# Four graph layers on one core: the variance from scaled squares, and softmax divisors applied to the attend's result

## The chip, the core and the metric

The kernel runs on 1 core of one Trainium2 chip. Its time is the device time of one execution in microseconds (us); several executions are given by their median. TensorE (PE) does the matmuls and writes PSUM, which has 8 banks; VectorE (DVE) and ScalarE (ACT) read PSUM and SBUF; GpSimd (POOL) works on SBUF here; SyncE (SP) issues nearly all DMAs.

## The reference

The input x has 128 batches of 128 nodes with 512 features, float32. Each of four layers is wrapped in a residual layernorm. `adj` is a sparse 128 x 128 matrix.

```python
x = _layernorm(x + adj @ x @ W0 + bias0)                      # layer 0
h = x @ W1                                                    # layer 1: graph attention
e = leaky_relu(s1[:, :, None] + s2[:, None, :]) * adj         # s1, s2 = h @ a1, h @ a2
x = _layernorm(x + elu(softmax(e, axis=2) @ h + beta * h))
A = adj @ x; C = A + b                                        # layer 2, edge maximum
x = _layernorm(x + max over the last axis of relu(A[:, :, None, :] + (C - A)[:, :, :, None]))
q, k, v = x @ w_qkv, 8 heads of 64                            # layer 3: masked attention
p = softmax(where(adj == 0, -inf, q @ k.T / 8))
o = (p @ v) @ w_proj + b_proj
x = _layernorm(x + o + (layernorm(o) * gamma + beta3))
```

The layernorm has eps = 1e-5. In layer 2 the value added is one number for each node (the maximum over the features of `adj @ x` plus b, at least 0).

## The kernel before

Every batch is a chain of steps in Python (`batch`, a generator), and so are the steps shared by two batches (pairs: `layer0`, `layer1`, `projection`) or four (groups: `section`, `tiled`). A chain asks for an engine with an assumed duration (`use("ACT", 0.48)`), for arena buffers of 256 columns (105 units; `SIZES` and `CAPS` say how large and how many of a kind) and for PSUM banks. A planner (`Plan`) runs all chains against each other when the program is built and emits the instructions of each engine in the order that this gives. Nothing is reordered on the chip: each engine executes its fixed list, and waits where a semaphore is not yet set. The constants at the top (ranks, `SLACK`, `LATE`, `RUN`, `SUMS3`, `SOON`, `KEPT`) bend this order. `RUN` holds a batch until the group that many before it has its layer-3 input; `SUMS3` is the rank of the additions that prepare sums of the layer-3 weights on POOL; a lower rank goes first. `KEPT` is how many last batches stay in SBUF and are not spilled to HBM between the layers.

The products with 512 x 512 weights use a seven-product scheme in place of eight (`seven`): POOL makes differences of input blocks (L919), PE multiplies 128 x 256 pieces (L932 for pairs, L981 for groups), ACT and DVE bring them out of PSUM (L823, L817, L811, L829). The first 14 batches and the last 4 use plain products in some places.

A layernorm is `layernorm_sums`: the row sum comes out of the step before it as an accumulator; DVE negates the mean (L346, L348), ACT squares and sums (L351), ACT divides and adds eps (L353), POOL takes the power -0.5 (L317), ACT multiplies mean and root (L356) and normalizes (L357). It runs four times a batch, but for the very last.

Layer 3 after the scores (L1060, one bank for four heads): DVE adds the mask as it reads PSUM (L1252), takes the maxima of 8 heads (L1260); ACT takes the 8 exps with their sums (L1274); DVE inverts the sums (L1281) and divides the last two heads (L1283), ACT the other six (L1289); DVE transposes 32 x 32 blocks (L1293), and the probabilities go through HBM to finish the transpose (`p_d`, L433 and L437). `attends` (L1081) then leaves the heads' result, transposed, in one bank: a partition is a feature of a head, a column is a node. ACT copies it out (L1324), which frees the bank, and the projection follows. `tiled` puts on PE, without a gap, the scores of two batches, the attends of an earlier group's four, and the scores of two more.

Of the kernel before, what the change touches and what calls it, by code (L numbers as in the profile page):

```python
# [19 lines left out]
APART = 4  # L20
FIRST = 0
PAIRS = 2
SOON = (-2, 2, -4, 10, 6, 18)
WHOLE = 0
KEPT = 6
ATTENDS = 2
RUN = 6
SEVEN0 = 1
SUMS2 = 1
SUMS0 = 0  # L30
SUMS3 = 12
ATTENDS_FIRST = 0
SCALED = 6
# [7 lines left out]
PROJ = -6  # L41
# [3 lines left out]
H = 8  # L45
# [10 lines left out]
CAPS = {"x": 9, "xr": 2, "yT": 8, "v": 4, "qk": 10, "xT": 4}  # L56
SIZES = {"u": 1, "t": 2, "x": 2, "early": 2, "xr": 2, "yT": 2, "v": 4, "qk": 4, "xT": 4}
LAST, AHEAD = 20, 4
# [3 lines left out]
LATE = 1.6  # L62
HANDOFF = {"PE": 0.2, "DVE": 0.13, "ACT": 0.16, "POOL": 0.09, "SP": 0.05}
DVE_ = 1.0
ACT_ = 1.02
POOL_ = 1.0
SP_ = 1.1
# [172 lines left out]
def gnn_stack_kernel(  # L240
# [90 lines left out]
    def layernorm_dve(xb):  # L331
        mv, rstd = yield from mean_rstd(xb)
        yield use("DVE", 0.59)
        nc.vector.tensor_scalar(xb, xb, mv[:, 0:1], rstd, op0=ALU.subtract, op1=ALU.mult)

    def row_sums():

        n = small.tile([P, 7], F32, name="sums", bufs=16)
        return [n[:, c : c + 1] for c in range(7)]

    def layernorm_sums(xb, total, unread, pieces=2):

        total, nm, squares, ve, rstd, nmr, more = total
        yield use("DVE", 0.07, follow=True)
        if unread or pieces == 1:
            nc.vector.tensor_scalar(nm, total, -1.0 / D, None, op0=ALU.mult)  # L346
        else:
            nc.vector.tensor_scalar(nm, total, more, -1.0 / D, op0=ALU.add, op1=ALU.mult)  # L348
        got = yield use("ACT", 1.03, lambda: () if unread else ("t",))
        unread = unread or got  # L350
        nc.scalar.activation(buf_or_bank(unread), xb, AF.Square, bias=nm, accum_out=squares)  # L351
        give(unread)
        nc.scalar.activation(ve, squares, AF.Identity, bias=eps, scale=1.0 / D)  # L353
        yield from root(ve, rstd)
        yield use("ACT", 1.03)
        nc.scalar.activation(nmr, nm, AF.Identity, scale=rstd)  # L356
        nc.scalar.activation(xb, xb, AF.Identity, bias=nmr, scale=rstd)  # L357
# [86 lines left out]
    eps = const.tile([P, 1], F32, name="eps")  # L444
    nc.gpsimd.memset(eps, EPS)
# [200 lines left out]
    class Group:  # L646


        def __init__(self, first, size):
# [10 lines left out]
            self.heads, self.o, self.sc, self.scratch = {}, {}, {}, {}  # L660
            self.eT, self.xT, self.slot, self.left = {}, {}, {}, {}
# [365 lines left out]
    def tiled(gr, before, bs):  # L1027
        yield gr.qk
        waiting = list(range(before.size)) if before else []
        for b in waiting:  # L1030
            yield before.rows[b]

# [33 lines left out]
    def attend(gr, bs):  # L1066
        for b in bs:
            yield gr.rows[b]
        slots = yield use(
# [40 lines left out]
    def batch(i):  # L1110
# [16 lines left out]
        if SEVEN0 and not direct:  # L1127
# [7 lines left out]
            gr.biased[h][j], gr.total[h][j] = biased, (total[0], total[6])  # L1135
# [3 lines left out]
            yield from layernorm_sums(xb, total, None)  # L1139
# [69 lines left out]
        yield from layernorm_sums(xb, total, unread)  # L1209
# [9 lines left out]
        yield use("DVE", 0.12)  # L1219
        nc.vector.tensor_scalar(mx, mx, b2_sb, 0.0, op0=ALU.add, op1=ALU.max)  # L1220
        if SUMS2:
            yield use("ACT", 0.71)
            total = row_sums()
            nc.scalar.activation(xb, xb, AF.Identity, bias=mx, accum_out=total[0])
            yield from layernorm_sums(xb, total, None, 1)
        else:
            yield use("ACT", 0.61)
            nc.scalar.activation(xb, xb, AF.Identity, bias=mx)
            yield from layernorm_dve(xb)
# [48 lines left out]
        short = (1.0 - SCALED / H) * 1.13  # L1278
        yield use("DVE", 0.18 + short + 0.11 * (SCALED < H), port=0.18 + short if short else None)
        rs = small.tile([P, H], F32, name="rs3")  # L1280
        nc.vector.reciprocal(rs, sums)  # L1281
        if SCALED < H:
            nc.vector.tensor_tensor(  # L1283
                pr[:, SCALED:], pr[:, SCALED:],
# [258 lines left out]
```

## Time and profile before

| | us |
|---|---|
| median of 3 runs | 2962.75 (2962.27 to 2963.49) |
| the profiled execution | 2962.69 |
| its span, first to last instruction | 2960.9 |
| PE, DVE, ACT, POOL busy | 2932.6, 2334.8, 2390.1, 1832.6 |
| granted TensorE clock, mean | 0.998 |

Busy time is the union of an engine's instructions. DMA engines are busy 53% of the span over all queues, moving 430.32 MB. A group's mean duration can be longer than the time between its neighbours' starts, because an instruction may begin before the one ahead of it has reported its end; matmuls of 128 x 256 are reported at 380 ns, and eight of them take 1.73 us.

### The profile page before, as it was taken

Reading aid. Unit: us, or ns where it says so; the run is one execution under the profiler, and the core shown is the slowest. Engines: PE = TensorE matmul, PEld = TensorE weight load, DVE = VectorE, ACT = ScalarE, POOL = GpSimd, SP = SyncE. Lnnn points to the kernel's source line nnn. Section 1 sums busy time; section 2 is a strip of 40 time slices with the busy share of each in tenths; the row PEclk is TensorE's granted clock in tenths of the full one; section 3 lists DMA queues with packets and bytes.
Section 4 is the critical chain, followed back from the end, with each engine's and each line's share of the span. In section 5 each row is a group of like instructions: output and inputs, shape, how many; then the busy total and the mean of one; then the engine's idle time right before and its main releaser. Section 6 shows DMA issues by size and latency. Waiting matters only on the chain. (4 is left out here: it accounts for less than half of the span.)

```text
span 2960.9 us, 55267 instructions
## 1 busy us (share of the span) xinstructions
PE 2932.6 (99%) x16503; PEld 2476.2 (84%) x16503; DVE 2334.8 (79%) x5758; ACT 2390.1 (81%) x7430; POOL 1832.6 (62%) x2045
## 2 busy tenths in 40 slices
PE   9999999999999999999999999999999999999998
PEld 5788888888888888888888888888888888888886
DVE  6897778787878778877878788777778778887767
ACT  5789868887877888887887888888888787887967
POOL 7854655574655665655666576665667566574545
PEclk9999999999999999999999999999999999999999
DMA  6535555463654564655545473654556547464435
GB/s 229 124 91 145 161 145 148 135 176 83 172 160 127 159 159 131 168 142 146 156 128 156 121 196 109 178 139 133 167 142 171 128 124 182 136 161 112 126 86 161
DMA packets 879882, 430.32 MB, mean 145 GB/s; under 512 B 567904, under 2 KB 781536, under 8 KB 879584
## 3 DMA queue, kind: packets, MB, share of 16 engines
q1 hardware_dynamic: 861152, 393.23, 49.4%
q10 hardware_dynamic: 18432, 33.56, 3.0%
q8 instruction: 133, 2.18, 0.3%
q14 instruction: 165, 1.35, 0.2%
HBM read 222.10 MB, written 204.54 MB: 144 GB/s over the span
## 5 line engine op out<-in xcount | busy, mean ns | idle before, releaser
L919 POOL TENSOR_TENSOR arena<-arena 128x256 f32<-128x256 f32 (+1 forms) x864 | 746.2, 870 | 387.8 <-PE ps L932 101.6
L317 POOL TENSOR_TENSOR sums<-sums,neghalf 128x1 f32<-128x1 f32 x511 | 329.2, 645 | 530.7 <-ACT sums L353 523.5
L932 PE MATMUL ps<-wsum_sb,arena 128*128 128x256 f32 x2196 | 543.8, 380 | 7.4 <-POOL arena L919 3.0
L932 PEld LDWEIGHTS ps<-wsum_sb,arena 128*128 128x128 f32 x2196 | 413.1, 190 | 89.4 <-issue 20.8
L981 PE MATMUL ps<-arena,wqkv_sb 128*128 128x256 f32 (+1 forms) x2112 | 479.4, 373 | 0.2 <-POOL arena L919 0.2
L932 PE MATMUL ps<-w_sb,arena 128*128 128x256 f32 x1936 | 478.9, 379 | 0.5 <-ACT arena L823 0.5
L823 ACT COPY arena<-ps 128x256 f32<-128x256 f32 (+1 forms) x892 | 336.2, 394 | 159.3 <-PE ps L932 78.2
L981 PEld LDWEIGHTS ps<-arena,wqkv_sb 128*128 128x128 f32 x2112 | 392.1, 190 | 65.1 <-issue 13.2
L351 ACT ACTIVATE arena<-arena,sums 128x512 f32<-128x512 f32 x497 | 355.5, 715 | 96.4 <-DVE sums L346 54.8
L817 DVE TENSOR_TENSOR arena<-ps,arena 128x256 f32<-128x256 f32 (+1 forms) x669 | 292.2, 452 | 176.8 <-ACT arena L823 89.3
L357 ACT ACTIVATE arena<-arena,sums 128x512 f32<-128x512 f32 x511 | 415.8, 814 | 17.1
L932 PEld LDWEIGHTS ps<-w_sb,arena 128*128 128x128 f32 x1936 | 366.0, 190 | 72.0 <-issue 19.9
L1274 ACT ACTIVATE arena<-arena,nmx 128x128 f32<-128x128 f32 x1024 | 402.9, 400 | 2.9 <-DVE nmx L1260 2.7
L981 PE MATMUL ps<-arena,wsum_sb 128*128 128x256 f32 (+1 forms) x1584 | 358.6, 373 | 1.1 <-POOL arena L919 1.1
L981 PEld LDWEIGHTS ps<-arena,wsum_sb 128*128 128x128 f32 x1584 | 293.3, 190 | 50.6 <-issue 7.9
L1289 ACT ACTIVATE arena<-arena,rs 128x128 f32<-128x128 f32 x768 | 278.3, 401 | 5.7 <-DMA x_d<-arena 1.1
L981 PE MATMUL ps<-wqkv_sb,arena 128*128 128x256 f32 x1024 | 241.3, 379 | 0.0
L363 POOL TENSOR_TENSOR arena<-arena,beta_sb 128x512 f32<-128x512 f32 x128 | 171.8, 1343 | 105.4 <-DVE arena L1235 97.8
L932 PE MATMUL ps<-wproj_sb,arena 128*128 128x256 f32 x992 | 236.1, 382 | 0.0
L1163 DVE SCALAR_TENSOR_TENSOR arena<-arena,wa_rows 128x512 f32<-128x512 f32 x256 | 208.4, 822 | 32.2 <-ACT arena L357 28.6
L981 PEld LDWEIGHTS ps<-wqkv_sb,arena 128*128 128x128 f32 x1024 | 194.1, 190 | 33.3 <-issue 6.0
L932 PEld LDWEIGHTS ps<-wproj_sb,arena 128*128 128x128 f32 x992 | 186.1, 190 | 31.5 <-issue 3.7
(117 smaller groups left out, 5375.1 us busy)
## 6 DMA issues: line engine op xcount, KB each, us to landing
p_d<-arena SPq DMA_DIRECT2D x256, 256.0 KB
arena<-p_d SPq DMA_DIRECT2D x128, 512.0 KB
x_d<-arena SPq DMA_DIRECT2D x242, 256.0 KB
arena<-x_d SPq DMA_DIRECT2D x968, 64.0 KB
arena<-in_x SPq DMA_DIRECT2D x127, 256.0 KB
out<-arena ACTq DMA_DIRECT2D x127, 256.0 KB
x_s<-arena SPq DMA_DIRECT2D x122, 256.0 KB
arena<-x_s SPq DMA_DIRECT2D x122, 256.0 KB
```

Of the source, the lines that this page charges most:

```text
L317: nc.gpsimd.tensor_tensor(rstd, ve, neghalf, op=ALU.pow)
L351: nc.scalar.activation(buf_or_bank(unread), xb, AF.Square, bias=nm, accum_out=squares)
L357: nc.scalar.activation(xb, xb, AF.Identity, bias=nmr, scale=rstd)
L363: nc.gpsimd.tensor_tensor(dst, dst, other, op=ALU.add)
L817: nc.vector.tensor_tensor(c, a, c, op=ALU.add)
L823: nc.scalar.copy(c, a)
L919: nc.gpsimd.tensor_tensor(blocks(out), blocks(a), blocks(b), op=ALU.subtract)
L932: nc.tensor.matmul(p, t[:, k], w[:, k, :], start=first and k == 0, stop=final and k == 1, skip_group_check=True,)
L981: nc.tensor.matmul(to, lhs, rhs, start=first and j == 0 and k == 0, stop=final and k == 1, skip_group_check=True,)
L1163: nc.vector.scalar_tensor_tensor(unread, xb, 1.0, wa_rows[:, j, :], op0=ALU.mult, op1=ALU.mult, accum_out=gr.s[:, b, j : j + 1],)
L1274: nc.scalar.activation(pr[:, j, :], pr[:, j, :], AF.Exp, bias=nmx[:, j : j + 1], accum_out=sums[:, j : j + 1],)
L1289: nc.scalar.activation(pr[:, j, :], pr[:, j, :], AF.Identity, scale=rs[:, j : j + 1])
```

## The change

The **variance**: the square is taken of the row scaled by 512^-0.5, with the negated mean scaled alike, so that the accumulator is the variance itself. DVE then adds eps and DVE multiplies mean and root; both were ACT's. **Layer 2**: its row constant is no longer added to the whole row by ACT. The layernorm before it sums its own output while it writes it, and the constant goes into the mean alone (`after`). The **attends** get undivided exps. The inverted sums of two batches are transposed by DVE, written to HBM (`r_d`), and loaded again so that every partition of a head holds that head's divisors along its columns (`divisors`; buffer kind "d", 4 units, one for each pair). DVE multiplies the attend's result by them as it leaves PSUM. The load is issued when all rows of the group are there (`divide`). The last 2 batches (`EARLY`) divide ahead of the attend as all did, four heads on each engine, and have the copy by ACT.

Constants of the planner change as well: weight sums later (`SUMS3`), 9 groups in place of 6 (`RUN`), 8 buffers x in place of 9, 7 batches kept, the last batch's exps in one instruction (`WHOLE`), attends of the last 3 groups apart in place of 4 (`APART`), other ranks and assumed durations.

```diff
-APART = 4
+APART = 3
-SOON = (-2, 2, -4, 10, 6, 18)
-WHOLE = 0
-KEPT = 6
+SOON = (-2, 2, -4, 12, 6, 18)
+WHOLE = 1
+KEPT = 7
-RUN = 6
+RUN = 9
-SUMS2 = 1
+EARLY = 2
-SUMS3 = 12
+SUMS3 = 24
-SCALED = 6
+SCALED = 4
-PROJ = -6
+PROJ = -4
-CAPS = {"x": 9, ...
+CAPS = {"x": 8, ...
-LAST, AHEAD = 20, 4
+LAST, AHEAD = 22, 4
-LATE = 1.6
+LATE = 1.8
-DVE_ = 1.0
+DVE_ = 1.04
-POOL_ = 1.0
-SP_ = 1.1
+POOL_ = 0.98
+SP_ = 1.0
...
+    def layernorm_sums(xb, total, unread, pieces=1, after=None, total_out=None):
+        total, nm, var, rstd, nmr, more = total
+        if after is None:
+            yield use("DVE", 0.07, follow=True)
+            if pieces == 1:
+                nc.vector.tensor_scalar(nm, total, -1.0 / D * D**-0.5, None, op0=ALU.mult)
...
         else:
-            nc.vector.tensor_scalar(nm, total, more, -1.0 / D, op0=ALU.add, op1=ALU.mult)
-        got = yield use("ACT", 1.03, lambda: () if unread else ("t",))
+            yield use("DVE", 0.2, follow=True)
+            nc.vector.tensor_scalar(nm, total, -1.0 / D, after, op0=ALU.mult, op1=ALU.subtract)
+            nc.vector.tensor_scalar(nm, nm, after, D**-0.5, op0=ALU.add, op1=ALU.mult)
+        got = yield use("ACT", 0.72, lambda: () if unread else ("t",))
...
-        nc.scalar.activation(buf_or_bank(unread), xb, AF.Square, bias=nm, accum_out=squares)
-        nc.scalar.activation(ve, squares, AF.Identity, bias=eps, scale=1.0 / D)
-        yield from root(ve, rstd)
-        yield use("ACT", 1.03)
-        nc.scalar.activation(nmr, nm, AF.Identity, scale=rstd)
-        nc.scalar.activation(xb, xb, AF.Identity, bias=nmr, scale=rstd)
+        nc.scalar.activation(
+            buf_or_bank(unread), xb, AF.Square, bias=nm, scale=D**-0.5, accum_out=var
+        )
+        yield use("DVE", 0.07, urgent=True)
+        nc.vector.tensor_scalar(var, var, EPS, None, op0=ALU.add)
+        yield from root(var, rstd)
+        yield use("DVE", 0.07, urgent=True)
+        nc.vector.tensor_scalar(nmr, nm, rstd, D**0.5, op0=ALU.mult, op1=ALU.mult)
+        if total_out is None:
+            yield use("ACT", 0.7)
+            nc.scalar.activation(xb, xb, AF.Identity, bias=nmr, scale=rstd)
+        else:
+            yield use("ACT", 0.78)
+            nc.scalar.activation(xb, xb, AF.Identity, bias=nmr, scale=rstd, accum_out=total_out)
...
-        yield from layernorm_sums(xb, total, unread)
+        sums2 = row_sums()
+        yield from layernorm_sums(xb, total, unread, total_out=sums2[0])
...
-            yield use("ACT", 0.71)
-            total = row_sums()
-            nc.scalar.activation(xb, xb, AF.Identity, bias=mx, accum_out=total[0])
-            yield from layernorm_sums(xb, total, None, 1)
+        yield from layernorm_sums(xb, sums2, None, after=mx)
...
+        for b in waiting:
+            done(before.divide[b // 2])
...
+        if i >= NB - EARLY:
...
+        else:
+            yield use("DVE", 0.12)
+        if i < NB - EARLY and h not in gr.rs:
+            gr.rs[h] = small.tile([P, 2, H], F32, name="rs3", bufs=6)
+            plan.start(divisors(gr, h), i)
+        if i < NB - EARLY:
+            nc.vector.reciprocal(
+                gr.rs[h][:, b % 2].rearrange("p (c j) -> p j c", j=2),
+                sums.rearrange("p (j c) -> p j c", j=2),
+            )
+            done(gr.summed[h])
...
-        nc.scalar.copy(oT, p)
+        if i >= NB - EARLY:
+            p, ba, v = gr.o.pop(b)
+            yield use("ACT", 0.48, urgent=True)
+            nc.scalar.copy(oT, p)
+        else:
+            yield gr.divided[h]
+            p, ba, v = gr.o.pop(b)
+            yield use("DVE", 0.6, urgent=True)
+            nc.vector.tensor_tensor(oT, p, gr.divisor[h][:, b % 2], op=ALU.mult)
+            gr.read(("d", h), 2)
...
+    def divisors(gr, h):
+        yield gr.summed[h]
+        bt = yield use("DVE", 0.62, "t")
+        st = buf(bt, 2, H, S)
+        nc.vector.transpose(
+            st, gr.rs.pop(h)[:, :, :, None].to_broadcast([P, 2, H, S])
+        )
+        row = dram.tile([2 * H, Q, S], F32, name="r_d", bufs=8)
+        yield use("SP", 0.4, late=2.0)
+        nc.sync.dma_start(
+            row.rearrange("e a r -> a e r"), st[::S].rearrange("p b h s -> p (b h) s")
+        )
+        give(bt)
+        if gr.first < firsts[-APART]:
+            yield gr.divide[h]
+        slot = gr.slot["d", h] = yield use("SP", 0.8, "d", late=2.6)
+        gr.divisor[h] = buf(slot, 2, K, P)
+        heads = row.rearrange("(e j) a r -> j e (a r)", j=2)
+        for j in range(2):
+            nc.sync.dma_start(
+                gr.divisor[h][j * HD : (j + 1) * HD].rearrange("p b c n -> p (b c) n"),
+                heads[j][None].to_broadcast([HD, 2 * K, P]),
+            )
+        done(gr.divided[h])
```

## The prediction

> **What bounds the kernel now.** I read the page first, then the waits of TensorE (PE), then the stretches, then the groups of ScalarE (ACT) and VectorE (DVE) by shape, then the timeline of the end. The page's first lines say that PE decides:
>
> ```profile
> span 2960.9 us, 55267 instructions
> ...
> PE 2932.6 (99%) x16503; PEld 2476.2 (84%) x16503; DVE 2334.8 (79%) x5758; ACT 2390.1 (81%) x7430; POOL 1832.6 (62%) x2045
> ```
>
> The reader is to see that PE is covered 99% of the time while no other engine is over 81%. The change touches no matmul, so the 2932.6 us stay. What can be won is PE's uncovered time, 2960.9 - 2932.6 = 28.3 us, and the little that it runs at a lower clock. The waits of PE say how thin this is:
>
> ```profile
> PE ps L1214 <- ACT arena L357: 4.6, 5, 1.7
> PE ps L932 <- ACT arena L823: 3.4, 3, 2.0
> PE ps L932 <- POOL arena L919: 3.0, 2, 1.7
> PE ps L370 <- ACT arena L1324: 1.9, 1, 1.9
> ```
>
> Columns: total us, times, longest. ACT ends most of it: the layernorm's last step (L357), the evacuation (L823), the attend's copy (L1324). The stretches say where; per engine they give the busy us:
>
> ```profile
> 90.00:115.00 25.00, 22.36 (x98) 17.00 (x97) 21.16 (x69) 22.13 (x55) 23.58 (x26) 1.00 0.60 141
> 115.00:145.00 30.00, 26.03 (x109) 20.41 (x108) 25.28 (x80) 25.87 (x68) 25.24 (x29) 0.94 0.42 93
> 200.00:300.00 100.00, 100.00 (x517) 83.31 (x516) 75.94 (x182) 95.01 (x288) 52.42 (x59) 1.00 0.54 145
> 2900.00:2920.00 20.00, 20.00 (x176) 17.69 (x176) 13.98 (x31) 19.08 (x73) 4.56 (x7) 1.00 0.53 160
> 2920.00:2940.00 20.00, 18.00 (x111) 11.63 (x109) 16.96 (x38) 12.01 (x38) 15.88 (x17) 1.00 0.65 196
> ```
>
> The columns are length, then PE, weight load, DVE, ACT, POOL, granted clock, DMA share, GB/s. **Early** (90 to 145 us) PE lacks 2.64 + 3.97 = 6.6 us, and 6% of the clock over 30 us is another 1.8: 8.4 us, with DVE, ACT and POOL all at 84 to 94%. **The end** lacks 2.0 us in 2920 to 2940 and some 1.85 in the next ten. The last matmul ends about 10.3 us before the span does; that tail is last(), which is not edited. The start is 1.4 us. That leaves 28.3 - 1.4 - 6.6 - 3.85 - 10.3 = 6.1 us for the **middle**, over 2700 us. So about 20 us are within reach (8.4 + 6.1 + 3.85 and some 1.7 of slow clock at the end), 0.7% of the time.
>
> The timeline of the end shows the slow clock: the same eight matmuls before and after a wait of 1.86 us.
>
> ```profile
> 2934.49 3.60 PE L370 MATMUL ps<-wproj_sb,arena 128*128 128x512 f32 x8
> ...
> 2941.85 5.40 PE L370 MATMUL ps<-wproj_sb,arena 128*128 128x512 f32 x8 [1.86 <-ACT arena L1324]
> ```
>
> The wait of 1.86 us was followed by 1.8 us of slow matmuls, so a wait here costs up to twice its length. The Trainium skill (TensorE: Matmul & The Clock Gate, Part 1: The HAM clock gate) puts the drop to half rate after an idle window of about 3.4 us; by it waits of 2 us would be free of that second cost, the end would hold 3.85 us and not 5.5, and my gain below would be 0.9 us smaller. The row is what I use.
>
> **The change, part by part.** The groups by shape that I price with (count, busy us, mean ns, idle before):
>
> ```profile
> L1289 ACT ACTIVATE arena<-arena,rs 128x128 f32<-128x128 f32 x768 | 278.3, 401 | 5.7 <-DMA x_d<-arena 1.1 <-DMA arena<-x_d 0.9 <-ACT arena L823 0.8
> L353 ACT ACTIVATE sums<-sums,eps 128x1 f32<-128x1 f32 x511 | 150.5, 294 | 16.6
> L356 ACT ACTIVATE sums<-sums 128x1 f32<-128x1 f32 x511 | 147.8, 289 | 58.9 <-POOL sums L317 56.2 <-ACT arena L823 0.7 <-issue 0.2
> L1224 ACT ACTIVATE arena<-arena,mx 128x512 f32<-128x512 f32 x128 | 91.5, 715 | 22.3 <-DVE mx L1220 20.4 <-DVE logits L764 1.4 <-DVE arena L1163 0.2
> L1324 ACT COPY arena<-ps 128x512 f32<-128x512 f32 x128 | 72.2, 581 | 50.1 <-PE ps L1081 49.9
> ```
>
> *ACT loses* all of L353 and L356 (150.5 + 147.8), L1224's activation (91.5; its accumulator read moves to L357), L1289 but for 8 of its 768 (275) and 126 of 128 copies (71): 736 us, so ACT falls from 2390 to about 1654 us, 56%. Rows of neighbours overlap a little, so less in occupancy, perhaps 670. ACT is off the bound; the worth lies where PE waited for it.
>
> *DVE gains.* Tiny 128x1 instructions are reported at 143 ns (L346) and 206 ns (L1220, with a pointer), but the timeline has their successors start 70 and 130 ns later, which is what they occupy. Per layernorm one of each, the added epsilon and the negated mean times the reciprocal root: 511 x 0.07 = 36 and 511 x 0.13 = 66. Layer 2's mean becomes two instructions, about 0.33 for 0.07: 128 x 0.26 = 33. The attend's result is multiplied as it leaves PSUM, nearest row L1252 (128x512 from PSUM, 680 ns, successive starts about 0.6): 126 x 0.6 = 76. A 128x512 transpose per pair (L1235, 706 ns, about 0.62): 63 x 0.62 = 39. L1283 goes: 128 x 0.42 = -54. Sum +196: DVE 2335 to about 2531 us, 85.5%. Bounds: if the small ones occupied their whole rows, 511 x (0.143 + 0.206) = 178 for 102, 88%; if each hid behind its neighbour, 82%. The Trainium skill (VectorE: DVE Perf Modes, The TRN2 errata) speaks against this step: every small instruction pays a fixed cost, put there at about 150 cycles of 0.96 GHz as measured. By that the 1022 small ones would take some 160 us, an estimate from that page, and DVE would stand at 87.5%. The starts in the trace are closer, so I keep 85.5%.
>
> Does DVE at 85.5% hold PE up? The row of 200 to 300 us has ACT at 95% with PE at 100.00 of 100: an engine nearly full costs nothing when the order is planned ahead of it. Against it, early there is no lead: 18 layernorms run in 90 to 145 (L357's counts, 7 and 11), adding 18 x 0.2 + 5 x 0.26 = 4.9 us to DVE's 46.4 of 55: 93%. ACT falls there by some 12 of 48.
>
> *Early, 8.4 us.* Layernorms lose a queue turn on ACT, and layer 2 goes from the maximum straight to the squares, without L1224's 0.72 us and its accumulator read. SUMS3 = 24 lets the additions of later batches go before the 16 weight sums on POOL (L595; 19.5 of POOL's 38.4 us in 50 to 90), though the sums must still run before the first section; one x buffer less holds a batch back. I take -5; bounds 0 + 8 (DVE full) and -8.
>
> *Middle, 6.1 us.* L357 ends the two longest waits (near 2458 and 140 us); the shorter chain takes 2.5 off. New waits for DVE: +1.5 taken, by the 95% row; bounds 0 and +15.
>
> *End, 5.5 us.* ACT is at 19.08 of 20 in 2900 to 2920; of this stretch's exps and scalings, 24 scalings in 2900 to 2940 (8.6 us) become 8, and the last batch's eight exps become one over the whole tile with two more DVE passes. The last scores' way to the last attend gets 3 to 6 us shorter, worth at most the 5.5: I take -3, bounds 0 and -5.
>
> *Divisors through HBM.* 63 writes and 126 broadcast loads of 256 KB, 32 MB on 430: DMA from 53% to about 57%. SP issues three more per pair at 0.37 to 0.57 us (rows of s_d), 1.3 us in 46. They run beside the probabilities' own way (transposes, p_d out and in) and are priced at nothing while they land before the attend ends. Behind the wait stands DVE's multiplication, in order, and with it every DVE evacuation queued after it; the attend's bank stays held.
>
> Sum: -5 - 2.5 + 1.5 - 3 = -9. The profiled execution took 2962.69 us (1.8 outside its span) and the median is 2962.75: **2953.7, say 2954**. A measurement of this kernel tells 0.2%, 5.9 us, from no change: faster means under 2956.8, slower over 2968.7.
>
> **Rivals.** (1) *Gains and new waits cancel*: early DVE at 93% gives nothing back, the end gives 3, the middle adds 2: 2957 to 2968. For it: POOL at 94% early, which is not relieved as a whole. (2) *Divisors land late, slower*: the load is released only when the group's rows are all there, just before score and attend (1.98 + 3.65 us). p_d's load at 2931.7 had its attend start at 2938.0, 6.3 us. If the broadcast takes as long, the first attends' banks stay some 2.5 us longer, and the multiplication blocks DVE's queue. Where this exceeds what the other banks cover, PE stands; at 0.5 to 1 us for each of 32 groups it is +16 to +32: 2970 to 2986 after the gains at the lower end. It decides from a landing later than 3.8 us after release, when two batches are scored and the first two attended (1.98 + 1.82 us). Against it: the order knows this time and can place other work. (3) *DVE becomes the bound*: its in-order waits add to 85.5%, and early and at the group borders PE waits for evacuations (L817, L829): +15 to +25 against -9, 2969 to 2979. For it: DVE at 89% in 145 to 200 already, though PE was full there.
>
> **How the numbers follow.** Forecast 0.49, its own range 2946 to 2956.8; (1) 0.19; (2) 0.18; (3) 0.14. Faster 0.49, same 0.19, slower 0.32. The range reaches from 2945 (the 20 us nearly all won) to 2983, leaving out the worst third of (2) and a little on top of the gains.
>
> **What would show it.** Right: ACT near 56 to 58%, DVE near 85%, PE's idle in 90 to 145 at 3 us or less, no wait of DVE for DMA at the new multiplication, L370 without its 1.86 us wait. Wrong: waits of PE for DVE over 5 us in all; DVE idle before the multiplication ended by the divisors' DMA; PE's idle in the middle over 10 us.

## The result, and the profile after

The changed kernel takes 2981.6 us (median of 4 runs, 2979.85 to 2985.33) against 2963.12 for the kernel before in the same runs: a ratio of 1.0063, with a 95% interval of 1.0051 to 1.0076. It is slower by 0.6%, where 2954 us had been forecast. The profiled execution took 2979.85 us. The first lines of its page:

```profile
span 2978.1 us, 55051 instructions
...
PE 2936.7 (99%) x16503; PEld 2472.8 (83%) x16503; DVE 2478.5 (83%) x6973; ACT 1766.6 (59%) x5379; POOL 1816.7 (61%) x2044
```

ACT lost 623.5 us and DVE gained 143.7, as planned, and the span still grew by 17.2 us. PE's busy time grew by 4.1, its idle time by 13.1. Where, by stretches of the span (idle us of PE; e1_narrow is an experiment told below):

| | 0 to 90 | 90 to 145 | 145 to 300 | 300 to 2800 | 2800 to end | sum |
|---|---|---|---|---|---|---|
| before | 1.54 | 6.62 | 0 | 6.05 | 14.05 | 28.3 |
| after | 5.26 | 1.14 | 0.44 | 16.65 | 17.94 | 41.4 |
| e1_narrow | 4.62 | 0.54 | 0.37 | 8.33 | 17.86 | 31.7 |

The middle, which had 6 us to give, lost 10.6 more. The waits of PE (total us, times, longest) name what came in:

```profile
PE ps L944 <- POOL arena L931: 6.9, 6, 1.9
PE ps L408 <- DMA arena<-in_x: 6.1, 4, 3.0
PE ps L381 <- ACT arena L1347: 6.0, 1, 6.0
PE ps L1231 <- ACT arena L368: 2.1, 6, 0.8
```

Three things are new against the table of before. PE waits for loads of x (`in_x`, L408), which it never noticeably did. Its wait for POOL's differences (L944 for L931; before, L932 for L919) has grown from 3.0 to 6.9 us. And the wait ahead of the end's L381 (L370 before) has grown from 1.9 to 6.0. The early stretch (90 to 145 us) did what was forecast and better; busy us of PE, weight load, DVE, ACT and POOL, then granted clock, DMA share and GB/s:

```profile
90.00:115.00 25.00, 24.55 (x120) 20.12 (x119) 21.86 (x73) 16.54 (x39) 22.65 (x26) 1.00 0.40 81
115.00:145.00 30.00, 29.31 (x134) 23.61 (x133) 27.29 (x109) 21.49 (x53) 26.45 (x33) 1.00 0.44 103
```

Now one of the new stalls in the middle, from three views of the changed kernel. The timeline of the queue of SP (start us, us), which issues the loads:

```profile
1679.97 4.08 SPq L1392 DMA_DIRECT2D arena<-r_d  x4
1684.14 0.57 SPq L493 DMA_DIRECT2D arena<-in_x  x1
```

The timeline of PE:

```profile
1689.20 1.10 PE L408 MATMUL ps<-arena,adjT 128*128 128x512 f32 x2 [2.98 <-DMA arena<-in_x]
```

And the stretches around it:

```profile
1680.00:1684.00 4.00, 4.00 (x20) 3.52 (x19) 3.21 (x16) 1.97 (x6) 0.93 (x2) 1.00 0.47 149
1684.00:1690.00 6.00, 3.02 (x13) 2.10 (x12) 2.54 (x5) 2.35 (x4) 2.62 (x3) 1.00 1.04 289
```

The four divisor loads of a group (L1392, 4 x 256 KB = 1 MB) go out together. The load of x that a later layer 0 needs stands behind them in the same queue. For 6 us the DMA engines are fully busy (share 1.04, 289 GB/s, where the whole span has a mean of 156), the x arrives late, and PE stands for 2.98 us. No other engine is near full in that stretch, and nobody waits there for the divisors themselves.

A second path may be POOL's. Its waits for the spilled rows, before (L919) and after (L931):

```profile
POOL arena L919 <- DMA arena<-x_d: 31.1, 9, 6.1
```

```profile
POOL arena L931 <- DMA arena<-x_d: 92.5, 17, 16.6
```

These are loads as well. That PE's longer wait for L931 follows from them is a guess at this point. The theory after this reading, **"loads"**: the 32 MB of divisors, issued in bursts of 1 MB, delay the loads queued behind them. Its rival, **"DVE"**: the extra 144 us of in-order work on DVE shifts evacuations and with them everything else. A third, **"order"**: the constants of the planner were fitted to other work, and a different list of instructions is simply a worse list.

### The profile page after: what moved, and what is told of

It reads as the page before. It is cut to its first block, busy times and chain, and to the rows that moved or that the text cites. A ratio compares the mean times of both kernels' runs of the same rounds, so it can differ in the third digit from the quotient of the medians.

```text
span 2978.1 us, 55051 instructions
## 1 busy us (share of the span) xinstructions
PE 2936.7 (99%) x16503; PEld 2472.8 (83%) x16503; DVE 2478.5 (83%) x6973; ACT 1766.6 (59%) x5379; POOL 1816.7 (61%) x2044
## 2 busy tenths in 40 slices
DMA packets 950404, 463.33 MB, mean 156 GB/s; under 512 B 574172, under 2 KB 852316, under 8 KB 950108
## 4 chain that ended last, share of the span: by engine, by line
PE 76%; DVE 8%; POOL 6%; DMA 3%; issue 3%; ACT 2%; SPq 2%; POOLq 0%; ACTq 0%; DVEq 0%
PE ps L993 32%; PE ps L944 28%; PE ps L1074 3%; PE ps L389 3%; PE ps L1231 3%; PE ps L1097 3%; PE ps L408 2%; POOL arena L374 2%; POOL arena L931 2%; POOL sums L317 1%; SPq L430 1%; DMA arena<-in_x 1%; DVE arena L1179 1%; DVE arena L829 1%; PE ps L381 1%
## 5 line engine op out<-in xcount | busy, mean ns | idle before, releaser
L931 POOL TENSOR_TENSOR arena<-arena 128x256 f32<-128x256 f32 (+1 forms) x864 | 725.8, 850 | 477.0 <-DVE arena L1352 112.3
L944 PE MATMUL ps<-wsum_sb,arena 128*128 128x256 f32 x2196 | 543.0, 380 | 8.7 <-POOL arena L931 6.9
L354 ACT ACTIVATE arena<-arena,sums 128x512 f32<-128x512 f32 x497 | 356.9, 718 | 246.0 <-DVE sums L342 98.9
L944 PEld LDWEIGHTS ps<-wsum_sb,arena 128*128 128x128 f32 x2196 | 412.9, 190 | 92.0 <-issue 18.8
L993 PE MATMUL ps<-arena,wqkv_sb 128*128 128x256 f32 (+1 forms) x2112 | 477.9, 373 | 0.0
L944 PE MATMUL ps<-w_sb,arena 128*128 128x256 f32 x1936 | 477.7, 379 | 0.0
L993 PEld LDWEIGHTS ps<-arena,wqkv_sb 128*128 128x128 f32 x2112 | 392.0, 190 | 62.8 <-issue 11.0
L944 PEld LDWEIGHTS ps<-w_sb,arena 128*128 128x128 f32 x1936 | 365.7, 190 | 68.6 <-issue 16.5
L365 ACT ACTIVATE arena<-arena,sums 128x512 f32<-128x512 f32 x383 | 307.6, 812 | 155.0 <-DVE sums L362 136.7
L993 PE MATMUL ps<-arena,wsum_sb 128*128 128x256 f32 (+1 forms) x1584 | 355.2, 373 | 0.4 <-POOL arena L931 0.3
L993 PEld LDWEIGHTS ps<-arena,wsum_sb 128*128 128x128 f32 x1584 | 293.1, 190 | 46.0 <-issue 6.2
L993 PE MATMUL ps<-wqkv_sb,arena 128*128 128x256 f32 x1024 | 242.0, 379 | 0.3 <-DVE arena L823 0.3
L944 PE MATMUL ps<-wproj_sb,arena 128*128 128x256 f32 x992 | 239.2, 382 | 1.0 <-DVE arena L1352 1.0
L993 PEld LDWEIGHTS ps<-wqkv_sb,arena 128*128 128x128 f32 x1024 | 193.9, 190 | 32.9 <-issue 5.2
L1179 DVE SCALAR_TENSOR_TENSOR arena<-arena,wa_rows 128x512 f32<-128x512 f32 x256 | 210.5, 829 | 10.2 <-ACT arena L365 4.5
L944 PEld LDWEIGHTS ps<-wproj_sb,arena 128*128 128x128 f32 x992 | 185.3, 190 | 33.6 <-issue 4.2
L374 POOL TENSOR_TENSOR arena<-arena,bproj_sb 128x512 f32<-128x512 f32 x124 | 163.2, 1325 | 68.6 <-ACT arena L835 56.2
L1284 ACT ACTIVATION_READ_ACCUMULATOR arena<-arena,nmx 128x1 f32 x1016 | 199.4, 196 | 0.0
```

Of the source, the lines that this page charges most:

```text
L374: nc.gpsimd.tensor_tensor(dst, dst, other, op=ALU.add)
L931: nc.gpsimd.tensor_tensor(blocks(out), blocks(a), blocks(b), op=ALU.subtract)
L944: nc.tensor.matmul(p, t[:, k], w[:, k, :], start=first and k == 0, stop=final and k == 1, skip_group_check=True,)
L993: nc.tensor.matmul(to, lhs, rhs, start=first and j == 0 and k == 0, stop=final and k == 1, skip_group_check=True,)
L1179: nc.vector.scalar_tensor_tensor(unread, xb, 1.0, wa_rows[:, j, :], op0=ALU.mult, op1=ALU.mult, accum_out=gr.s[:, b, j : j + 1],)
L1284: nc.scalar.activation(pr[:, j, :], pr[:, j, :], AF.Exp, bias=nmx[:, j : j + 1], accum_out=sums[:, j : j + 1],)
```

## Experiments

The difficulty is that the order is planned when the program is built: a changed assumed duration anywhere gives another list. So the sharpest kernels here keep the list of the changed kernel (or of before) and change only the size of an operand, the layout or the queue of a transfer, or add one. In e1, e5, e10, e11 and e13 the traces hold the instructions of every engine in the same order as in the changed kernel; so do e9 and e12 (e12 against the kernel before), but for the transfers that are moved or added.

**e1_narrow: the same list, less divisor data.** Each load fills 8 partitions of 64; the rest of the divisor tile is not written, so the attend's result is multiplied by stale values.

```diff
-                gr.divisor[h][j * HD : (j + 1) * HD]...
-                heads[j][None].to_broadcast([HD, 2 * K, P]),
+                gr.divisor[h][j * HD : j * HD + 8]...
+                heads[j][None].to_broadcast([8, 2 * K, P]),
```

> The changed kernel with the order of every engine's instructions kept, but each broadcast load of the divisors reaches 8 of its 64 partitions (32 KB in place of 256 KB, 28 MB less in all; the other partitions are multiplied by whatever lies there, so the result is left out of account). Theory DMA (the added transfers delay the loads of x and x_d that stand behind them, and PE ends up waiting for those): PE's waits for arena<-in_x fall from 6.1 us to under 1.5, POOL's wait for arena<-x_d from 92.5 us towards the 31 us of before, PE's idle between 300 and 2800 us from 16.6 to about 7, the time by some 9 us to about 2972. Theory DVE (DVE's 143 us more of work makes PE late): nothing changes, 2980 to 2984. Theory order (the fixed order is simply less lucky): nothing changes either.

Measured: 2968.04 us, ratio to before 1.0018 [1.0008, 1.0027]. That is 13.6 us below the changed kernel; 10.5 between the two profiled spans. The page, and the waits of PE and of POOL:

```profile
PE 2935.9 (99%) x16503; PEld 2476.9 (83%) x16503; DVE 2479.5 (84%) x6973; ACT 1768.5 (60%) x5379; POOL 1820.1 (61%) x2044
```

```profile
PE ps L381 <- ACT arena L1347: 6.0, 1, 6.0
PE ps L944 <- POOL arena L931: 3.8, 3, 1.9
...
PE ps L408 <- DMA arena<-in_x: 1.5, 2, 1.3
```

```profile
POOL arena L931 <- DMA arena<-x_d: 52.0, 12, 14.5
```

DVE is as busy as in the changed kernel, with the same instructions, and the slowdown is gone but for 5 us: this is the loads. The same place in its SP timeline (it falls 4 us earlier), and the 6 us from the issue of x on, which in the changed kernel were those of 1.04:

```profile
1676.47 2.50 SPq L1392 DMA_DIRECT2D arena<-r_d  x4
1679.06 0.36 SPq L493 DMA_DIRECT2D arena<-in_x  x1
```

```profile
1679.00:1685.00 6.00, 6.00 (x28) 4.90 (x27) 4.04 (x11) 3.12 (x6) 3.57 (x4) 1.00 0.77 238
```

The load of x leaves 2.59 us after the first divisor load, not 4.17, and meets DMA engines that are less full. In the landing records of the two traces it then lands 2.90 us after its issue (at 1681.96), not 4.92 (at 1689.06). So at this place 1.6 us of the delay are SP's issue and 2.0 the transfer. Both shrink together: a median load takes SP 304 ns to issue and not 632. How the 13.6 us divide between the two, this kernel doesn't tell.

POOL's waits are a weaker sign than they look. Under the name x_d they fall from 92.5 to 52.0 us, but 12.5 us come up under r_d and 21.3 under the load of e_d; over all loads and stores, POOL waits at L931 for 118.4 us in the changed kernel and 102.8 here. What does fall with the time are PE's own waits.

**e13_half: 32 of the 64 partitions** (the same edit with 32 for 8; the other half stale).

> The changed kernel, same order of every engine, each broadcast load of the divisors to 32 of its 64 partitions (128 KB; the other half is multiplied by what lies there). If the cost grows with the bytes, half of the narrow loads' gain of 13.6 us (which was for 7/8 of the bytes) comes: 4/7 of it, 7.8 us, so 2971 to 2977. If only a whole burst blocks, near 2981; if the number of issues counts and not the bytes, near 2981 too.

Measured: 2969.8 us, 1.0022 [1.0013, 1.0031]. Its wait of PE for x:

```profile
PE ps L408 <- DMA arena<-in_x: 1.2, 2, 0.7
```

Half the bytes give back 11.8 of the 13.6 us, where in proportion it would have been about 8, so the cost is no price per byte. It looks like a threshold: what counts is whether a load that PE needs comes too late, and with the half bursts it mostly does not. Here too both shrink, the bytes and SP's issue (448 ns a load).

**e5_contiguous: the same bytes and list in larger pieces.** The divisors are laid out so that each partition reads one run of 4 KB and not eight of 512 bytes.

```diff
-        heads = row.rearrange("(e j) a r -> j e (a r)", j=2)
+        heads = row.rearrange("(j e) a r -> j (e a r)", j=2)
...
-                heads[j][None].to_broadcast([HD, 2 * K, P]),
+                heads[j][None].to_broadcast([HD, 2 * K * P]),
```

> The changed kernel with the same order of every engine and the same bytes, but the inverted sums are laid down so that the 8 rows of 128 that one partition loads follow each other in HBM: each broadcast load is 64 pieces of 4 KB in place of 512 of 512 B (504 in place of 4032 packets per engine group, 56,000 fewer in all). If what delays the loads behind it is the number of pieces (issue and packets), most of the 13.6 us that the narrow loads won comes back: 2968 to 2973, and PE's waits for arena<-in_x fall under 3 us. If it is the bytes (32 MB through the same 16 engines), nothing moves: 2979 to 2984.

Measured: 2985.4 us, 1.0071 [1.0056, 1.0086], with 893,956 packets in place of 950,404. No gain: the number of pieces is not the cause. (SP's issue hardly changes, 588 ns a load for 632.)

**e12_before_bytes: the opposite direction.** The kernel before, with four extra copies of 256 KB for each group on SP at the place where the group's attends begin (`tiled`), from x to a scratch tensor in HBM that nobody reads: 460.74 MB in all, near the changed kernel's 463.33. DVE, ACT, PE and POOL keep their lists.

```diff
+        for b in waiting:
+            nc.sync.dma_start(dram.tile([P, D], F32, name="none", bufs=16), x[before.first + b])
```

> The kernel before with the divisors' traffic alone: when a group's rows are there, SP issues four copies of 256 KB from the input to a scratch in HBM (31 groups, 32.5 MB) that nobody reads; all other instructions and their order as before. Theory bytes: 8 to 14 us more than before, 2970 to 2977, with PE waiting for arena<-in_x or POOL for arena<-x_d. If the order of before has room for the traffic: within 3 us of 2962.8, and the bytes hurt only where the change's order left the loads late.

Measured: 2971.81 us, 1.0033 [1.0021, 1.0044], 8 us above before; PE's idle in 300 to 2800 us goes from 6.05 to 12.55. Copies in bursts harm the old kernel as well, with nothing else changed, and by some 60% of what the divisors cost in the new one. The way that the expectation gave for it does not show, though. No wait of PE for in_x is over the 0.3 us of before, and POOL's wait for x_d is shorter than the 31.1 us of before:

```profile
POOL arena L919 <- DMA arena<-x_d: 26.7, 10, 5.0
```

PE's idle time grows in small pieces, most of them put down to POOL, ACT and an attend. So e12 shows that such traffic costs time in another list too, and not by which wait.

**e9_act_queue: the divisor loads are issued by ACT**, which has become free, so that x and x_d don't stand behind them on SP.

```diff
-            nc.sync.dma_start(
+            nc.scalar.dma_start(
```

> The changed kernel with the divisors' broadcast loads issued by ACT in place of SP, same bytes, same place in the emission; PE, DVE, POOL and the rest of SP keep their order. If the loads of x and x_d are late because they stand behind the divisors in SP's own queue, most of the 13.6 us that the narrow loads won comes back: 2968 to 2974, PE's waits for arena<-in_x under 2 us. If it is the DMA engines' bandwidth, which all queues share, little moves, and ACT's blocked issue can add: 2978 to 2988.

Measured: 2996.46 us, 1.0120 [1.0103, 1.0137], worse than any expectation. The first two lines are from the waits of PE, the third from those of DVE:

```profile
PE ps L408 <- DMA arena<-in_x: 1.4, 2, 0.8
...
PE ps L1074 <- DVE arena L1352: 4.8, 2, 3.9
```

```profile
DVE arena L1352 <- DMA arena<-r_d: 16.7, 9, 5.6
```

The wait for x falls from 6.1 to 1.4, which fits that a good part of it was the place behind these loads in SP's queue. But the loads now reach the multiplication late (16.7 us of waits, where the changed kernel has 6.6), DVE blocks there, and PE waits for it: here rival (2) of the prediction takes place. Of the 16.3 us that its span is longer than the changed kernel's, 8.1 are idle time of PE; the other 8.2 are PE's busy time, with a mean clock of 0.995 for 0.998. The Trainium skill (DMA: Bandwidth & Descriptors, Rules for kernel authors) says that spreading the issue over several engines doesn't help the bandwidth and only saves issue time; e9, which won nothing by it, does not speak against that, and adds what it costs on the other side: 126 issues of a median 611 ns, by that some 77 us of ACT's queue, in an order that had not planned for them.

**e10_dve_light: the rival "DVE", tested alone.** The multiplication takes one of the attend's four blocks of 128 columns, and the divisors' transpose one head of eight; the rest of the results is left out. Loads and list are unchanged.

```diff
-            nc.vector.tensor_tensor(oT, p, gr.divisor[h][:, b % 2], op=ALU.mult)
+            nc.vector.tensor_tensor(oT[:, :1], p[:, :1], gr.divisor[h][:, b % 2, :1], op=ALU.mult)
...
-            st, gr.rs.pop(h)[:, :, :, None].to_broadcast([P, 2, H, S])
+            st[:, :, :1], gr.rs.pop(h)[:, :, :1, None].to_broadcast([P, 2, 1, S])
```

> The changed kernel with DVE's new large instructions cut down (the multiplication of the attend's result to 1 of 4 feature blocks, the divisors' transpose to 1 of 8 heads; the rest of both is left out), all orders, waits and bytes kept. DVE's busy time falls by some 80 us to about 2400. Theory DVE (its load makes PE late): 5 to 9 us less, 2973 to 2977. Theory bytes: within 2 us of 2981.6.

Measured: 2981.33 us, 1.0062 [1.0047, 1.0077]. Its page, and the stretch of 1500 to 2000 us in it, in the changed kernel, in e1_narrow and in e12_before_bytes:

```profile
PE 2938.7 (99%) x16503; PEld 2474.5 (83%) x16503; DVE 2414.6 (81%) x6973; ACT 1769.0 (59%) x5379; POOL 1819.5 (61%) x2044
```

```profile
1500.00:2000.00 500.00, 493.19 (x2802) 418.74 (x2802) 407.15 (x1181) 289.60 (x869) 304.99 (x350) 1.00 0.58 156
```

```profile
1500.00:2000.00 500.00, 493.17 (x2823) 418.21 (x2822) 418.94 (x1182) 288.52 (x867) 305.06 (x351) 1.00 0.58 155
```

```profile
1500.00:2000.00 500.00, 497.82 (x2853) 424.20 (x2852) 425.93 (x1194) 295.24 (x900) 307.09 (x351) 1.00 0.53 146
```

```profile
1500.00:2000.00 500.00, 498.47 (x2854) 425.96 (x2853) 396.88 (x984) 408.02 (x1289) 319.63 (x357) 1.00 0.58 159
```

64 us less on DVE change nothing: PE stands for 6.8 us of these 500 with or without them, and for 2.2 when the loads are small. So the large new instructions on DVE are not the cause. The 1022 small ones were not taken away in any run with this list; but e1 keeps them all and has lost all but 5 us of the slowdown, so no more than that is left to them.

**The end: e4, e6 and e11.** PE's wait of 5.96 us ahead of the last batches' projection is ended by ACT's copy (L1347). *e4_end_copy_dve* gives this copy to DVE, *e6_end_first* lets the planner put it ahead of two layernorm pairs on ACT, *e11_end_pool_light* has POOL add only a quarter of the columns in the last 8 batches (the other columns keep what they held).

```diff
 e4:
-            yield use("ACT", 0.48, urgent=True)
-            nc.scalar.copy(oT, p)
+            yield use("DVE", 0.6, urgent=True)
+            nc.vector.tensor_copy(oT, p)
 e6:
-        yield use("SP", 0.43, late=4.0)
+        yield use("SP", 0.43, late=4.0 if i < NB - EARLY else 0.0)
 e11, and alike for the addition of o to xs[i]:
+            cut = slice(0, P if i >= NB - 8 else D)
+            plan.start(pool_add(o[:, cut], bproj_sb[:, cut], biased), i)
```

> The changed kernel with the last two batches' copies out of PSUM (L1347) on DVE in place of ACT; the order is the same up to the last 40 us. If PE's wait of 5.96 us at 2957.6 comes from ACT's order (the copies stand behind two layernorm instructions that wait for DVE, while ACT is idle), it falls to 2 us or less and with it the slow clock after it: 4 to 6 us less, about 2976. If the wait comes from DVE and POOL being behind with the last projections, DVE's copy is as late: within 1.5 us of 2981.

> The changed kernel with one assumed duration changed for the last two batches (the landing of their probabilities, 0 in place of 4.0), so that the planner puts their two copies out of PSUM (L1347) ahead of two layernorm pairs on ACT; all engines keep their order until the last 40 us. Theory of ACT's order: PE's wait of 5.96 us for L1347 falls under 1.5 us and the half clock after it shortens: 4 to 7 us less, 2975 to 2978. If PE's gap only moves to the next product, the time stays within 1.5 us of 2981.6.

> The changed kernel with POOL's additions of layer 3 cut to a quarter of their columns for the last 8 batches (the other columns are left out), orders kept; some 13 instructions of 1.3 us become 0.5. If the last 25 us are set by the chain of the last layernorms over POOL and DVE, and PE's wait of 6 us only shows it: 4 to 7 us less, 2975 to 2978. If they are set by PE and ACT's copies: within 1.5 us of 2981.6.

Measured: 2984.32 us, 1.0069 [1.0054, 1.0084]; 2980.7 us, 1.0058 [1.0042, 1.0075]; 2981.84 us, 1.0063 [1.0048, 1.0078]. None moves the time. e6 is the instructive one. The timelines of PE at the end, first of the changed kernel, then of e6 ("..." leaves out the last attends):

```profile
2942.66 7.03 PE L381 MATMUL ps<-wproj_sb,arena 128*128 128x512 f32 x16
...
2957.55 5.17 PE L381 MATMUL ps<-wproj_sb,arena 128*128 128x512 f32 x8 [5.96 <-ACT arena L1347]
2962.55 3.62 PE L1511 MATMUL ps<-wproj_sb,arena 128*128 128x256 f32 x16
```

```profile
2945.61 7.03 PE L381 MATMUL ps<-wproj_sb,arena 128*128 128x512 f32 x16
...
2955.08 3.70 PE L381 MATMUL ps<-wproj_sb,arena 128*128 128x512 f32 x8 [0.54 <-ACT arena L1347]
2958.62 3.62 PE L1511 MATMUL ps<-wproj_sb,arena 128*128 128x256 f32 x16
```

The wait is gone, so it came from the copies' place in ACT's list. Counted from the 16 matmuls of L381 that both have, PE ends 6.9 us earlier: 16.6 us after their start and not 23.5. But the span ends only 0.8 us earlier, 34.6 us after their start and not 35.4, and what comes after the last matmul grew from 11.9 to 18.0 us (10.2 in the kernel before). So the end is hardly set by PE, and PE's longest wait was mostly a sign. From 2940 to 2960 us the changed kernel has DVE and POOL nearly full:

```profile
2940.00:2960.00 20.00, 14.04 (x65) 8.08 (x64) 17.31 (x42) 4.15 (x9) 19.01 (x18) 0.84 0.38 118
```

A lighter POOL alone (e11: 10.0 in the same 20 us) wins no more: its span of 2981.4 us ends 34.5 us after the same matmuls.

```profile
2946.85 7.03 PE L381 MATMUL ps<-wproj_sb,arena 128*128 128x512 f32 x16
```

Which part of the chain of the last layernorms on DVE, POOL and ACT holds the end stays open; no run takes DVE's share of it away.

**The parts alone: e2 and e3.** *e2_variance_alone* sets `EARLY = 128`: every batch divides ahead of the attend, and no divisor goes through HBM (the inverted sums get 8 buffers in place of 2). *e3_attends_alone* keeps the divisors and puts back the layernorm and layer 2 of before.

```diff
 e2:
-EARLY = 2
+EARLY = 128
 e3: layernorm_sums and the code of layer 2 as in the kernel before
```

> The changed kernel with EARLY = 128: every batch divides ahead of its attend as the last two do (four heads on each engine), no divisors go through HBM, the copy is ACT's again; the scaled-square variance, layer 2 and all constants stay. The planner makes another order. Theory DMA: the middle's idle falls by about 10 us, the end stays; 2968 to 2973. Theory DVE: DVE keeps the small instructions and half of the divisions (its busy time close to 2440), so about half of the loss stays: 2972 to 2977. Theory order: anything within 10 us of 2981.

> The changed kernel with the layernorm and layer 2 of before (ACT divides, adds eps, multiplies mean and root, adds the row constant), undivided exps and divisors through HBM kept, all constants of the change kept. Theory DMA: the middle's idle stays at 14 us or more and PE still waits for arena<-in_x; 2978 to 2988. Theory DVE: DVE falls by some 130 us to about 2345 and the middle's idle with it to under 9 us; 2968 to 2974. Theory order: anything within 10 us of 2981.

Measured: 3006.34 us, 1.0144 [1.0123, 1.0165], and 3029.49 us, 1.0224 [1.0209, 1.0239]: each alone is slower than both together, outside every expectation. e2's longest wait of PE is a single one of 14.1 us for `p_d`, and it has one of 4.1 us for `in_x`, with no divisor load at all: another list can have PE wait for x for other reasons. e3 has DVE at 2370.3 us, less than the changed kernel, and is the slowest of all. Neither says what a part is worth: each has another list, with constants that were changed for both parts together.

**How much a list alone is worth: e7, e8, e14 to e18.** To see this, one assumed factor is moved by one or two hundredths (the factor on DVE's assumed durations, 1.04 after and 1.0 before), or a margin of the planner is set to 0.48. The computation stays the same; only the order differs. *e14* is e7's order with e1's narrow loads.

```diff
 e7:  -DVE_ = 1.04  +DVE_ = 1.03        e8:  -DVE_ = 1.0  +DVE_ = 1.01
 e16: -DVE_ = 1.04  +DVE_ = 1.05        e15: -DVE_ = 1.0  +DVE_ = 1.02
 e18: +MARGIN = 0.48 (after)            e17: +MARGIN = 0.48 (before)
```

> The changed kernel with the assumed factor on DVE's durations 1.03 in place of 1.04: the same work in another order, to see how far the order alone moves the time. If the order is of little weight: within 5 us of 2981.6. If the constants were found for just this order: 2985 to 3010.

> The kernel before with that factor 1.01 in place of 1.0, for the same question. If the order is of little weight: within 5 us of 2962.7. If the constants were found for just that order: 2967 to 2990.

> The changed kernel with the assumed DVE factor 1.03 (2992.6 with full loads) and the narrow loads of 8 partitions, so the order is that of e7_replan_after. If the bytes cost in any order: 8 to 15 us less, 2978 to 2985. If they cost only where the first order left the loads late: 2989 to 2994.

> The kernel before with the assumed DVE factor 1.02: a third order of the old work. After 3013 at 1.01, the theory that the constants were found for just one order expects 2980 to 3025; if 1.01 was a single bad draw, 2963 to 2975.

> The changed kernel with the assumed DVE factor 1.05: a third order of the new work. The theory that orders scatter by tens of us whatever the work expects 2985 to 3020; if the new work bears re-ordering better (ACT with room), 2978 to 2995.

> The kernel before with MARGIN 0.48 in place of 0.5, the time by which the planner lets PE's work be ready early: a fourth order of the old work. Scatter of orders: 2970 to 3025; little weight of the order: within 5 us of 2962.8.

> The changed kernel with MARGIN 0.48: a fourth order of the new work. Scatter of orders: 2980 to 3020; little weight of the order: within 5 us of 2981.6. If the changed work is slower as such, its mean over the orders but the first lies above that of before by 10 us or more; if the two chosen orders alone differ, the means lie within 10 us.

| order | kernel before, us | ratio | kernel after, us | ratio |
|---|---|---|---|---|
| as given | 2963.1 | 1 | 2981.6 | 1.0063 [1.0051, 1.0076] |
| one hundredth | e8: 3013.0 | 1.0168 [1.0147, 1.0188] | e7: 2992.6 | 1.0099 [1.0079, 1.0119] |
| the other step | e15: 2982.2 | 1.0062 [1.0042, 1.0082] | e16: 3002.1 | 1.0129 [1.0109, 1.0150] |
| margin | e17: 2977.7 | 1.0047 [1.0031, 1.0063] | e18: 2993.2 | 1.0097 [1.0068, 1.0127] |

Every neighbour is slower than the order given, by 15 to 50 us before and by 11 to 20 after. Over the three neighbours the means are 2991.0 and 2996.0 us, 5 apart with standard deviations of 19 and 5. So whether the changed computation is slower as such, these runs don't tell; with the lists as given it is. e14 took 2986.75 us, 1.0083 [1.0066, 1.0100], 5.9 below e7 and between its two expectations, but the two intervals overlap: in that order the loads cost less than 13.6 us, and the run doesn't measure how much. The names of POOL's waits mislead here as well. Under x_d they fall, as in e1, from 76.0 us in e7 to 36.1, but r_d comes up in e14 with what is missing:

```profile
POOL arena L931 <- DMA arena<-r_d: 38.9, 3, 15.5
POOL arena L931 <- DMA arena<-x_d: 36.1, 14, 15.4
```

## Why the prediction was wrong

**The step that failed** is "Divisors through HBM ... They run beside the probabilities' own way (transposes, p_d out and in) and are priced at nothing while they land before the attend ends." They did land in time: DVE waited for them at the multiplication only 7 times, 6.6 us in all.

```profile
DVE arena L1352 <- DMA arena<-r_d: 6.6, 7, 2.3
```

The price was paid by others, at the place shown by a load of x behind them. With the same list the term is +13.6 us (e1); like traffic in the list of before costs some 8 (e12). The issues were priced low as well: two loads and a write take SP some 1.8 us a pair by their medians (632, 632 and 561 ns), where 1.3 had been taken. What misled was "DMA from 53% to about 57%": correct as a mean, and no measure of a burst, which stood at 1.04 for 6 us. The argument "the order knows this time and can place other work" held for the multiplication, of which it was said, and did not cover the other loads. Rival (2) named the right object and had 2970 to 2986 us, in which the result lies, but by luck: its mechanism, the blocked multiplication, shows as a cost only in e9.

Between the profiled executions the forecast said -9 us and the span grew by 17.2. Of the 26 us in between, 10.5 are the loads (e1), and by e1's stretches 6.8 the end, 3.3 the middle, 3.3 PE's busy time, which was to stay as it was, and 2.4 the early part up to 300 us.

**The early term was right where it was looked at.** 90 to 145 us fell from 6.6 to 1.14 us of idle time and the clock from 115 rose from 0.94 to 1.00, so the -5 was reached. It was given back ahead of it: 0 to 90 has 3.7 us more idle time of PE, of which 50 to 90 has 2.1, with POOL at 38.75 of 40 us, as full as before; why, no run tells. Rival (1) had said "POOL at 94% early, which is not relieved"; the net is -1.8 us.

**The end term** was -3 and measured +3.9. The step "The last scores' way to the last attend gets 3 to 6 us shorter" looked at PE's wait as the bound. The wait of 1.86 us became one of 5.96, by the copies' place in ACT's list, and e6 shows that even without it the end moves by only 0.8 us.

**The middle term**, -2.5 and +1.5, is +2.3 in e1, where the loads are small: no gain, and in the bounds given. The -2.5 was too much to take: of the two waits named for it the one at 140 us lies in the early stretch, and in 300 to 2800 us L357 ended only 2.1 us of PE's waits in the kernel before. The large rest, +8.3, is the loads.

**The costs of instructions** held roughly. ACT is at 59% where 56 to 58 was expected; DVE gained 143.7 us where 196 was summed, and stands at 83%. The groups by shape (count, busy us, mean ns, idle before):

```profile
L1352 DVE TENSOR_TENSOR arena<-ps,arena 128x512 f32<-128x512 f32 x126 | 82.2, 680 | 11.8 <-DMA arena<-r_d 6.6 <-PE ps L1097 2.2 <-PE ps L993 1.5
L362 DVE TENSOR_SCALAR sums<-sums 128x1 f32<-128x1 f32 x511 | 103.8, 205 | 78.1 <-POOL sums L317 76.2
L359 DVE TENSOR_SCALAR sums<-sums 128x1 f32<-128x1 f32 x511 | 72.7, 143 | 57.5 <-ACT arena L354 52.2 <-ACT ps L354 3.7
L1377 DVE STREAM_TRANSPOSE arena<-rs 128x512 f32<-128x512 f32 x63 | 44.4, 704 | 1.4 <-DMA x_d<-arena 0.5
```

Multiplication and transposes have the durations of the nearest rows that were taken, 680 and 704 ns. The 1022 small ones occupy less than was taken: without L359 and L362 the union of DVE's instructions is 71 us shorter, where 102 had been taken; the 160 that the prediction sets beside it are further off. Rival (3), DVE as the bound, did not occur: PE's waits for DVE stay under 5 us, and e10 shows that 64 us of DVE's work are worth nothing here.

**Of the signs**, those for ACT, DVE and the early stretch came as for "right", and the middle's idle time of 16.65 us as for "wrong"; the wait of L370 (L381 now) did not go but grew. DVE's short waits at the multiplication came as well, but cost little. What the prediction did not price at all is the list itself, and a hundredth or two in one constant of the planner moves the time by more than any term in its sum. The remaining 5 us of e1 over before (span +6.7: end +3.8, middle +2.3, up to 300 us -2.6, PE's busy time +3.3) can't be put down to the computation or to the order by these runs, and why PE's busy time grew they don't tell either.

## What to carry to other kernels

Price a transfer that is "hidden" by the stretch in which its burst runs and by who stands behind it in the queue, not by the mean share of the DMA engines and not by its own deadline alone: its consumer may be on time and all others late. Where an order is planned from assumed costs, test a cause in an unchanged list by shrinking an operand or adding a transfer; undoing half of a change plans another list, and here lists alone scatter by 11 to 50 us. Relieving an engine, even by a quarter of its time, is worth only what the stretches show PE to lose to it.

## What was unexpected of the hardware

A wait of PE has a second cost in one execution and none in another. After 5.96 us at the end, the eight matmuls of L381 took 5.17 us (3.70 in e6 after 0.54 us), with the clock at 0.71 in the 6 us from 2957. After 2.98 us in the middle (at 1689), the pair of L408 took 1.10 us, where undisturbed pairs take 1.02 to 1.13, the eight of L993 behind it 1.89, and the clock stayed at 1.00. But at the same place of the same list e11 waited less and lost the clock, and its eight took 3.12 us. First the changed kernel, then e11:

```profile
1684.00:1695.00 11.00, 8.02 (x34) 6.02 (x33) 4.93 (x10) 3.94 (x7) 2.62 (x3) 1.00 0.97 276
1690.13 1.89 PE L993 MATMUL ps<-wsum_sb,arena 128*128 128x256 f32 x8
```

```profile
1684.00:1695.00 11.00, 8.33 (x30) 6.20 (x29) 4.28 (x12) 3.21 (x6) 3.55 (x4) 0.84 0.97 290
1690.59 1.60 PE L408 MATMUL ps<-arena,adjT 128*128 128x512 f32 x2 [2.67 <-DMA arena<-in_x]
1691.99 3.12 PE L993 MATMUL ps<-wsum_sb,arena 128*128 128x256 f32 x8
```

The Trainium skill (TensorE: Matmul & The Clock Gate, Part 1: The HAM clock gate) puts the drop after an idle window of about 3.4 us. The waits of 2.98 and 5.96 us fit that, taken as the length of a wait; those of 2.67 us in e11 and of 1.86 us that the prediction quotes, with 5.40 us for the eight after it, do not. So a wait of 2 to 3 us may cost nothing beside itself or about its own length again, and the prediction's "up to twice its length" is a bound in these cases and not a price.

The cost of a burst is not linear: half of the divisors' bytes cost 1.8 us over an eighth of them, with intervals that overlap, and the whole 11.8 over the half.
